# Row by row on ScalarE's queue: 33 of 1173 gathered tiles leave GpSimd in a graph network on one core

## The chip, the cores and the metric

The kernel runs on one core of a Trainium2 chip. The metric is the device time of one execution in microseconds, and the time before is the median of three runs. A core has five engines, each with a queue of instructions of its own that it takes in order: TensorE (PE, matrix products, with weight loads as PEld), VectorE (DVE), ScalarE (ACT), GpSimd (POOL) and SyncE (SP, which only starts transfers). A "q" behind an engine's name (ACTq, DVEq) stands for its sequencer, which loads registers, waits for semaphores and issues transfers.

## The reference

The program is a graph network of three layers over N = 6250 nodes with D = 256 features, and E = 100000 edges, each with a source, a destination, one of R = 3 relations and 32 attributes. Edges are sorted by destination.

```python
ew = edge_attr @ edge_w + edge_b                       # [E, 256], the same in all layers
inv_cnt[i] = 1 / max(number of edges of relation i that end in a node, 1)
for l in range(3):
    residual = x
    msg = relu(x[src] * ew)                            # a row of x for each edge
    out = 0
    for i in range(3):
        h = segment_sum(msg * (edge_type == i), dst)   # [6250, 256]
        out += (h * inv_cnt[i]) @ weights[l, i]
    out += x @ roots[l] + biases[l]
    x = residual + relu(out)
return layernorm(x_in + x)
```

The part that matters here is `x[src]`: for each edge, in each layer, one row of 256 floats (1 KB) has to come from the table x in memory, at an index known only at run time.

## The kernel before

**Tiles.** Edges are cut into tiles of 128. Two tiles are a pair, and a layer has 391 pairs. Two pairs share a room, a tile `xs` of 128 x 2 x 2 x 256 floats (`room`, 8 of them, so 16 pairs). The order of pairs in a layer is fixed in `schedule`. An inner loop runs over iterations `it`; in each, every step of the pipeline acts on a pair that is some places ahead or behind.

**One iteration, in the order of the program.** The whole kernel is written under a manual schedule: each engine does its own instructions in exactly this order.

- `gather` / `gather_pair` (L898 to L902) for the pair nine places ahead: two indirect transfers on POOL's queue. Each reads 128 indices from `src_io` and fetches 128 rows of 1 KB into half of a pair's place in the room. POOL does nothing else in the loop. A gather has to wait until the room's previous content has been reduced.
- Transfers on SP's queue: attributes `at` for eight pairs (L559), weights, and, where a block of nodes ends, its rows of x for the next layer (`x_mid`, L723) or the output.
- `reduce` (L640 to L647) for the current pair: PE multiplies the weighted rows `xs` by one-hot matrices `oh` into `h_p`, which has two buffers. With it, sums over edges become matrix products.
- `make_ew` (L594 to L606), in every fourth iteration: PE computes `ew` of four pairs into four banks `ew_p`.
- `add` (L649 to L659) for the pair before: DVE adds `h_p` to `acc`, at a place that it holds in a register. Registers are loaded eight at a time (L652, a TENSOR_LOAD on DVE's sequencer).
- `weigh` (L623 to L628), in every second iteration, for the room that is three pairs ahead: DVE multiplies each pair's 128 x 512 values by its `ew_p` (L626, reading and writing `xs`), and ACT does one relu over the room (L628).
- For each block of 128 nodes, spread over the iterations: `root_turn` (PE), `root_turned` (L668, an ACT copy `t_s`), `root_mul` (L672, PE) and `root_keep` (L675, DVE) for x @ roots; `node_mul` (L687, PE), `node_end` (L718, L721, DVE) and `clear` (L704, ACT) for the sums that are complete.
- `one_hot` (L630 to L638) for the room two places ahead: four DVE comparisons, and in layer 0 a copy on ACT (`oh_b`, L638).

ACT's queue carries few transfers in the loop: nine pieces of x (L545 to L548) and one block of indices (L564) in layer 0.

**Between layers.** The rows that layer l + 1 gathers are those that layer l has written to `x_mid`; the first pairs of a layer are gathered early and completed by `complete` (L612 to L621).

Of the kernel before, what the change touches and what calls it, by code (L numbers as in the profile page):

```python
# [8 lines left out]
F32 = mybir.dt.float32  # L9
BF = mybir.dt.bfloat16  # L10
I32 = mybir.dt.int32
# [431 lines left out]
def ordered_path(ctx, tc, x, attr_laid, A, weights, roots, biases, edge_w, edge_b, out, src, src_i, seg, place_i, consts, x_root,  # L443
# [6 lines left out]
    nc = tc.nc  # L450
    P = 128
    N, D = x.shape
# [10 lines left out]
    order, _, moved, least, most = schedule(N, E, 1)  # L463
# [19 lines left out]
    with tc.tile_pool(name="bias_s", bufs=1) as bias_s:  # L483
# [9 lines left out]
        rows_of = bias_s.tile([P, D], F32, name="rows_of")  # L493
# [34 lines left out]
    edge = ctx.enter_context(tc.tile_pool(name="edge", bufs=2))  # L528
# [7 lines left out]
    def first_of(p, n):  # L536
        return p == 0 or order[p - 1] // n != order[p] // n
# [19 lines left out]
    def load_at(g):  # L557
        at = edge.tile([P, GROUP // OCT, 2, P], F32, name="at", bufs=3)
        nc.sync.dma_start(at.rearrange("p o i e -> p (o i e)"), attr_laid[g])  # L559
        return at  # L560

    def find_came():
        e = 2 * P * order[0]
        nc.scalar.dma_start(came_i.rearrange("p t e -> p (t e)"),  # L564
                            src[e:e + 2 * FIRST * P][None, :].to_broadcast([P, 2 * FIRST * P]))
        for t in range(2 * FIRST):
            nc.vector.tensor_scalar(came[:, t, :], came_i[:, t, :], node_i[:, 0:1], None, op0=ALU.is_equal)

    def layer(l, r_sb, b_sb, ats, early, pools):
# [5 lines left out]
        x_rows = x if l == 0 else x_mid[l - 1]  # L575
        w_sb = wpool.tile([P, R * DC, D], F32, name="w_sb")
        CH = DC + 1 if l == 0 else DC
        xs, ew_ps, ohs, h_ps, o_ps, rs = {}, {}, {}, {}, {}, {}
        x0s, mvs, oh_bs, t_ss, places = {}, {}, {}, {}, []
        r_next, ats_next, early_next = (None, None), {}, {}  # L580

        def gather(u):
            p = order.index(u)
            if p < FIRST:
                xs[u // 2] = early[u // 2]
            else:
                if first_of(p, 2):
                    xs[u // 2] = room(rows, D)
                gather_pair(nc, xs[u // 2], x_rows, src_i, u)

        def pairs_of(q):
            return range(min(2, U - 2 * q))
# [15 lines left out]
        def gather_early(p):  # L608
            u = order[p]
            if first_of(p, 2):  # L610
                early_next[u // 2] = room(rows, D)
            gather_pair(nc, early_next[u // 2], x_mid[l], src_i, u)  # L612

        def complete(q):
            for k in pairs_of(q):
# [4 lines left out]
                                     start=True, stop=True)  # L620
                nc.vector.tensor_add(xs[q][:, k], rest, xs[q][:, k])  # L621

        def weigh(q, pairs=None):  # L623
            pairs = pairs_of(q) if pairs is None else pairs
            for k in pairs:
                nc.vector.tensor_mul(xs[q][:, k], ew_ps[2 * q + k], xs[q][:, k])  # L626
            there = xs[q][:, pairs.start:pairs.stop]
            nc.scalar.activation(there, there, AF.Relu)  # L628

# [112 lines left out]
        def load_x0(c):  # L742
            n = min(P, N - c * P)
            x0s[c] = edge.tile([P, D], F32, name="x0", bufs=2)
            if n < P:
                nc.vector.memset(x0s[c], 0.0)
            nc.sync.dma_start(x0s[c][:n, :], x[c * P:c * P + n, :])
# [12 lines left out]
        for it in range(-11, max(starts) + 7):  # L760
            def pair(k):
                return order[it + k] if 0 <= it + k < U else None
            if pair(AHEAD) is not None:
                gather(pair(AHEAD))
            if l < L - 1 and 0 <= it + AHEAD - U < FIRST:
                gather_early(it + AHEAD - U)
            if l == 0 and it == 20:
                find_came()
            if pair(AHEAD) is not None and pair(AHEAD) // GROUP not in ats:
                ats[pair(AHEAD) // GROUP] = load_at(pair(AHEAD) // GROUP)  # L770
            if l == 0 and it >= -4 and (it + 4) % 20 == 0 and (it + 4) // 20 * 6 < NT - 1:
                load_x((it + 4) // 20 * 6)
            if it == 10:
                nc.sync.dma_start(w_sb, weights[l].rearrange("r (c p) e -> p (r c) e", p=P))
            if l == L - 1 and it + 2 in root_at:
                load_x0(root_at[it + 2])
            if l < L - 1 and it == U - 10:
                r_next = load_root(l + 1)
            if l < L - 1 and U - 10 <= it < U - 8:
                ats_next[at_groups[it - U + 10]] = load_at(at_groups[it - U + 10])  # L780

            if pair(0) is not None:
                reduce(pair(0))
            if pair(4) is not None and first_of(it + 4, OCT):
                make_ew(pair(4) // OCT)
            if pair(-LAG) is not None:
                add(pair(-LAG))
            if pair(3) is not None and first_of(it + 3, 2):
                if l > 0 and it + 3 < FIRST:
                    complete(pair(3) // 2)  # L790
                if pair(3) // 2 != order[-1] // 2:
                    weigh(pair(3) // 2)

            if pair(3) is not None and pair(3) // 2 == order[-1] // 2:
                weigh(pair(3) // 2, range(pair(3) % 2, pair(3) % 2 + 1))
            if it in root_at:
                root_turn(root_at[it])
            if it - 1 in root_at:
                root_turned(root_at[it - 1])
            if it - 2 in root_at:  # L800
                root_mul(root_at[it - 2])
            if it - 3 in root_at:
                root_keep(root_at[it - 3])
            if it == moved:
                move()
            if it - 2 == moved:
                clear(P)
            if it + 1 in node_at and slot_of(node_at[it + 1]) == 0:
                wrap()
            if it in node_at:  # L810
                node_mul(node_at[it], 0)
            if it - 1 in node_at:
                node_end(node_at[it - 1], 0)
            if it - 2 in node_at:
                node_mul(node_at[it - 2], 1)
            if it - 3 in node_at:
                node_end(node_at[it - 3], 1)
                clear(slot_of(node_at[it - 3]))
            if it - 4 in node_at and l == L - 1:
                deviate(node_at[it - 4])  # L820
            if it - 5 in node_at and l == L - 1:
                norm(node_at[it - 5])
            if pair(2) is not None and first_of(it + 2, 2):
                one_hot(pair(2) // 2)
# [68 lines left out]
def room(rows, D):  # L893

    return rows.tile([128, 2, 2, D], F32, name="xs", bufs=ROWS)


def gather_pair(nc, xs, x_rows, src_i, u):  # L898
    for i in range(2):
        nc.gpsimd.indirect_dma_start(  # L900
            out=xs[:, u % 2, i, :], out_offset=None, in_=x_rows[:, :],
            in_offset=bass.IndirectOffsetOnAxis(ap=src_i[:, 2 * u + i:2 * u + i + 1], axis=0))  # L902
# [162 lines left out]
```

## Time and profile before

| | |
|---|---|
| median of 3 runs | 3694.33 us (3691.32 to 3695.99) |
| the profiled execution | 3692.14 us |
| its span | 3690.3 us |
| its mean granted TensorE clock | 0.843 |
| PE busy | 2687.3 us, 73% |
| DVE busy | 2082.3 us, 56% |
| ACT busy | 935.3 us, 25%, 1155 instructions |
| POOL busy | 2244.9 us, 61%, 2355 instructions |
| DMA, all queues | 387.87 MB, mean 105 GB/s; of that the gathers 307.65 MB |

The page gives for each engine its busy time and its share of the span; instructions of the sequencers are not counted as busy. A group in the page stands for one line, engine, operation and shape, with its number, its busy time, the mean time of one, and the idle time of the engine just before these instructions with what ended most of it. "Issue" as a releaser means that the engine waited for nothing that the profile shows. A releaser "remote" or "another core or an unknown queue" is a semaphore event whose source the profile could not place. PE's ends are modelled, and spans on POOL are rough.

### The profile page before, as it was taken

The page shows a single profiled execution, that of the slowest core. Times are in us where ns is not written, and L with a number is a line of the kernel's source. Part 1 is how long each engine was busy: PE and PEld are TensorE (multiplying, and loading weights), DVE is VectorE, ACT ScalarE, POOL GpSimd, SP SyncE. Part 2 cuts the span into 40 slices and gives each one's busy share as a digit, 9 for nine tenths or more (in the row PEclk, how much of TensorE's full clock was granted, in tenths as well). Part 3 has the DMA queues.
Part 4 walks back from the last instruction along what each step waited for, and adds up shares of the span by engine and source line. Part 5 has one row for each costly group of instructions (what it writes and reads, how often), then busy time and mean ns, then how long its engine had stood idle before and what let it go on. Part 6 is the DMA issues. An engine that isn't in the chain of part 4 may idle for free.

```text
span 3690.3 us, 54932 instructions
## 1 busy us (share of the span) xinstructions
PE 2687.3 (73%) x18875; PEld 2261.2 (61%) x18875; DVE 2082.3 (56%) x5868; ACT 935.3 (25%) x1155; POOL 2244.9 (61%) x2355
## 2 busy tenths in 40 slices
PE   3777877888886667777777777665777777777766
PEld 3666666666666556666666656555666666666655
DVE  4555655566665445555555555544555656666655
ACT  2233333333333222222222222211222222222221
POOL 5666665665566556666666666656666666666664
PEclk9788888888888778888889889787888888888887
DMA  4333333333333333333333333333333333333332
GB/s 129 117 109 119 106 111 98 102 106 103 100 107 106 98 90 100 98 104 104 104 100 106 107 107 104 104 96 112 109 113 113 106 109 111 105 105 107 107 105 67
DMA packets 173323, 387.87 MB, mean 105 GB/s; under 512 B 43418, under 2 KB 78636, under 8 KB 173036
## 3 DMA queue, kind: packets, MB, share of 16 engines
q0 software_dynamic: 112608, 307.65, 28.9%
q1 hardware_dynamic: 53136, 68.50, 5.7%
q10 hardware_dynamic: 7292, 8.11, 0.7%
q8 instruction: 154, 2.52, 0.3%
q14 instruction: 133, 1.09, 0.1%
HBM read 364.62 MB, written 19.46 MB: 104 GB/s over the span
## 4 chain that ended last, share of the span: by engine, by line
PE 49%; another core or an unknown queue 12%; DVE 11%; issue 8%; POOL 1%; DMA 1%; DVEq 1%; ACT 1%; POOLq 0%; ACTq 0%
PE h_p L644 27%; PE o_p L687 10%; PE ew_p L605 6%; DVE xs L626 4%; DVE acc L659 3%; PE r_p L672 3%; PE ew_p L601 2%; DVE x_root L718 2%; DVE oh L634 2%; POOL xs L900 1%; DMA xs<-x_mid,src_io 1%; PE r_p L664 1%; DVE x_all L721 0%; DVEq L659 0%
## 5 line engine op out<-in xcount | busy, mean ns | idle before, releaser
L644 PE MATMUL h_p<-oh,xs 128*128 128x120 f32 x9336 | 1544.9, 317 | 735.5 <-DVE acc L659 485.0
L900 POOL DMA_INDIRECT xs<-x_mid,src_io x1564 | 1497.1, 957 | 930.4 <-issue 810.2
L644 PEld LDWEIGHTS h_p<-oh,xs 128*128 128x128 f32 x9336 | 1400.5, 225 | 916.5 <-DVE acc L659 535.5
L626 DVE TENSOR_TENSOR xs<-ew_p,xs 128x512 f32<-128x512 f32 x1167 | 756.2, 682 | 871.4 <-PE h_p L644 340.3
L628 ACT ACTIVATE xs<-xs 128x1024 f32<-128x1024 f32 (+1 forms) x588 | 617.6, 1050 | 2396.8 <-DVE xs L626 2190.7
L900 POOL DMA_INDIRECT xs<-in_x_dram,src_io x770 | 734.1, 953 | 475.2 <-issue 413.0
L659 DVE TENSOR_TENSOR acc<-h_p,acc 128x240 f32 (+1 forms) x1173 | 518.1, 442 | 448.1 <-remote 255.6
L687 PE MATMUL o_p<-w_sb,acc 128*128 128x256 f32 (+1 forms) x1716 | 523.6, 446 | 109.5 <-DVE x_root L718 57.1
L634 DVE TENSOR_SCALAR oh<-iota_w,seg_o 128x120 f32<-128x120 f32 x2346 | 518.7, 295 | 0.0
L687 PEld LDWEIGHTS o_p<-w_sb,acc 128*128 128x128 f32 (+1 forms) x1716 | 359.0, 223 | 205.8 <-issue 62.9
L605 PE MATMUL ew_p<-ew_sb,at 32*128 32x256 f32 x4692 | 361.8, 426 | 4.4 <-issue 4.4
L605 PEld LDWEIGHTS ew_p<-ew_sb,at 32*128 32x128 f32 x4692 | 275.2, 220 | 42.3 <-issue 12.6
L718 DVE SCALAR_TENSOR_TENSOR x_root<-o_p,inv,x_root 128x256 f32<-128x256 f32 (+1 forms) x429 | 206.0, 480 | 121.6 <-PE o_p L687 42.6
L672 PE MATMUL r_p<-r_sb,t_s 128*128 128x256 f32 x588 | 185.2, 438 | 81.7 <-ACT t_s L668 68.4
L672 PEld LDWEIGHTS r_p<-r_sb,t_s 128*128 128x128 f32 x588 | 113.8, 216 | 104.5 <-ACT t_s L668 74.5
L638 ACT ACTIVATE oh_b<-oh 128x480 bf16<-128x480 f32 x196 | 117.8, 601 | 197.4 <-DVE oh L634 152.2
L704 ACT ACTIVATE acc<-zero_o 128x768 f32<-128x768 f32 (+1 forms) x150 | 140.8, 938 | 74.2 <-PE r_p L687 17.9
L601 PE MATMUL ew_p<-bias,full_ones 3*128 3x512 bf16 x1173 | 142.6, 453 | 21.4 <-issue 17.7
L644 PE MATMUL h_p<-oh_b,full_ones 128*128 128x120 bf16 x782 | 120.1, 238 | 10.0 <-issue 9.6
L644 PEld LDWEIGHTS <-full_ones 128*128 128x128 bf16 x782 | 89.8, 115 | 23.1 <-issue 17.1
L664 PE MATMUL r_p<-ident_o,x_all 128*128 128x128 f32 x294 | 73.2, 340 | 0.0
L675 DVE TENSOR_TENSOR x_root<-r_p,b_sb 128x256 f32<-128x256 f32 x147 | 61.1, 415 | 19.6 <-PE r_p L672 8.5
(92 smaller groups left out, 485.8 us busy)
## 6 DMA issues: line engine op xcount, KB each, us to landing
at<-in_attr_laid_dram SPq DMA_DIRECT2D x147, 256.0 KB
xs<-x_mid,src_io POOLq DMA_INDIRECT x1564
xs<-in_x_dram,src_io POOLq DMA_INDIRECT x770
x_mid<-x_all SPq DMA_DIRECT2D x96, 128.0 KB
x_all<-in_x_dram ACTq DMA_DIRECT2D x8, 768.0 KB
x<-in_x_dram SPq DMA_DIRECT2D x48, 128.0 KB
out_dram<-x_all SPq DMA_DIRECT2D x48, 128.0 KB
w_sb<-in_L_gnn_weights_dram SPq DMA_DIRECT2D x3, 768.0 KB
```

What stands on the lines that cost most here:

```text
L601: nc.tensor.matmul(banks[j].rearrange("p i d -> p (i d)"), full_ones[j * A:j * A + PARTS, :], bias[j * A:j * A + PARTS].rearrange("p i d - ...
L605: nc.tensor.matmul(banks[j][:, i, :], ats[OCT * o // GROUP][j * A:(j + 1) * A, o % (GROUP // OCT), i, :], ew_sb[j * A:(j + 1) * A, :], sta ...
L626: nc.vector.tensor_mul(xs[q][:, k], ew_ps[2 * q + k], xs[q][:, k])
L628: nc.scalar.activation(there, there, AF.Relu)
L634: nc.vector.tensor_scalar(ohs[q][:, t, :], iota_w, seg[:, 4 * q + t:4 * q + t + 1], None, op0=ALU.is_equal)
L644: nc.tensor.matmul(h_ps[u][:, d, :], xs[u // 2][:, u % 2, i, d * P:(d + 1) * P] if d < DC else full_ones, (ohs if d < DC else oh_bs)[u // ...
L659: nc.vector.tensor_tensor(there, h_ps[u][:, :CH].rearrange("p c (r w) -> p c r w", r=R), there, op=ALU.add)
L672: nc.tensor.matmul(rs[c][:, 1, :], t_ss[c][:, d, :], r_sb[:, d, :], start=(d == 0), stop=(d == DC - 1))
L687: nc.tensor.matmul(o_p[:n, j, :], acc[:, d, r, slot:slot + n], w_sb[:, r * DC + d, :], start=(d == 0), stop=(d == DC - 1))
L704: nc.scalar.activation(acc[:, :CH, :, slot:slot + P], zero[:, :, None, None].to_broadcast([P, CH, R, P]), AF.Copy)
L718: nc.vector.scalar_tensor_tensor(root, o_p[:n, j, :], inv[:n, c, r:r + 1], root, op0=ALU.mult, op1=ALU.add)
L900: nc.gpsimd.indirect_dma_start(out=xs[:, u % 2, i, :], out_offset=None, in_=x_rows[:, :], in_offset=bass.IndirectOffsetOnAxis(ap=src_i[:, ...
```

## The change

For 33 of the 1173 tiles of a run (11 in each layer) the gather on POOL is left out. Their rows come one by one: each row is a DMA of its own, 1 KB from the row of x that a register names to one partition of a tile `lent0` (128 x 256 floats, two buffers). ACT's queue issues them.

- `HANDS_OF` lists who fetches rows: one entry, ACT's queue, four rows in an iteration, two buffers.
- `lent_to` plans it: starting in iteration 6, each lent tile takes 32 iterations, one tile after the other. The tile chosen is the first one of a room whose pair stands at least 6 places behind the end of the fetch.
- `lend(it)` is called in each iteration right after `gather`. Four iterations before a tile's fetch begins, SP loads its 128 indices (512 bytes) to one partition. Then four row DMAs are issued in each iteration, and after every eighth row the next eight indices are loaded into ACT's registers. That makes 4224 row DMAs, 528 register loads and 33 index loads in all.
- `gather_pair` skips a lent tile, so one gather of that pair stays.
- `weigh` splits the product of a pair with a lent tile into two products of 128 x 256: the first reads `lent0` and writes to the room, the second works in the room as before. The relu is unchanged.

```diff
@@ layer
+        hands = [(queue, kind, rate, buffers, lent_to(order, N, P, j, rate))
+                 for j, (queue, kind, rate, buffers) in enumerate(HANDS_OF(nc))]
+        lent = {(q, k, i): None for hand in hands for _, q, k, i in hand[-1]}
+        indices, values = {}, {}
+
+        def lend(it):
+            for j, (queue, kind, rate, buffers, plan) in enumerate(hands):
+                for s, q, k, i in plan:
+                    if it == s - 4:
+                        e = (4 * q + 2 * k + i) * P
+                        indices[q] = edge.tile([1, P], I32, name=f"index{j}", bufs=2)
+                        nc.sync.dma_start(indices[q], src[e:e + P][None, :])
+                    if not s <= it < s + -(-P // rate):
+                        continue
+                    if it == s:
+                        lent[q, k, i] = edge.tile([P, D], F32, name=f"lent{j}", bufs=buffers)
+                    for r in range((it - s) * rate, min(P, (it - s + 1) * rate)):
+                        if r % 8 == 0:
+                            _, values[j] = nc.values_load_multi_w_load_instructions(
+                                indices[q][0:1, r:r + 8], engines=[kind], min_val=0, max_val=N - 1,
+                                skip_runtime_bounds_check_because="each source is a node")
+                        queue.dma_start(lent[q, k, i][r:r + 1, :], x_rows[bass.ds(values[j][r % 8], 1), :])
@@ gather
-                gather_pair(nc, xs[u // 2], x_rows, src_i, u)
+                gather_pair(nc, xs[u // 2], x_rows, src_i, u, lent)
@@ weigh
+        def parts(q, k):
+            return [(0, 1), (1, 1)] if any((q, k, i) in lent for i in range(2)) else [(0, 2)]
...
-                nc.vector.tensor_mul(xs[q][:, k], ew_ps[2 * q + k], xs[q][:, k])
+                for i, n in parts(q, k):
+                    there = xs[q][:, k, i:i + n]
+                    rows_of = lent.get((q, k, i))
+                    nc.vector.tensor_mul(there, ew_ps[2 * q + k][:, i:i + n],
+                                         there if rows_of is None else rows_of[:, None, :])
@@ the loop over it
                 gather(pair(AHEAD))
+            lend(it)
@@
+def lent_to(order, N, P, j, rate):
+    steps = -(-P // rate)
+    plan, s = [], 6 + 4 * j
+    while True:
+        p = s + steps + 6
+        while p + 1 < len(order) and (order[p] // 2 != order[p + 1] // 2 or order[p] // 2 == order[p - 1] // 2):
+            p += 1
+        if p + 12 > len(order):
+            return plan
+        q = order[p] // 2
+        plan.append((s, q, j, j))
+        s += steps
+
+def HANDS_OF(nc):
+    return ((nc.scalar, mybir.EngineType.Activation, 4, 2),)
+
+def gather_pair(nc, xs, x_rows, src_i, u, lent=()):
     for i in range(2):
+        if (u // 2, u % 2, i) in lent:
+            continue
         nc.gpsimd.indirect_dma_start(
```

More of the change, by code (lines that the diff above doesn't have):

```diff
@@ L895, in room @@
     return rows.tile([128, 2, 2, D], F32, name="xs", bufs=ROWS)
-def gather_pair(nc, xs, x_rows, src_i, u):
+def lent_to(order, N, P, j, rate):
[13 more added lines that the diff above has]
+def gather_pair(nc, xs, x_rows, src_i, u, lent=()):
     for i in range(2):
+        if (u // 2, u % 2, i) in lent:
+            continue
         nc.gpsimd.indirect_dma_start(
```

## The prediction

> **What bounds the kernel now.** The page is read first, by engine shares, by the chain that ended last and by the costliest groups.
>
> ```profile
> span 3690.3 us, 54932 instructions
> PE 2687.3 (73%) x18875; PEld 2261.2 (61%) x18875; DVE 2082.3 (56%) x5868; ACT 935.3 (25%) x1155; POOL 2244.9 (61%) x2355
> ...
> PE 49%; another core or an unknown queue 12%; DVE 11%; issue 8%; POOL 1%; DMA 1%; DVEq 1%; ACT 1%; POOLq 0%; ACTq 0%
> ...
> L900 POOL DMA_INDIRECT xs<-x_mid,src_io x1564 | 1497.1, 957 | 930.4 <-issue 810.2
> L626 DVE TENSOR_TENSOR xs<-ew_p,xs 128x512 f32<-128x512 f32 x1167 | 756.2, 682 | 871.4 <-PE h_p L644 340.3
> ...
> L900 POOL DMA_INDIRECT xs<-in_x_dram,src_io x770 | 734.1, 953 | 475.2 <-issue 413.0
> ```
>
> By these lines PE would be the bound and POOL idle for over a third. But 930.4 + 475.2 us of idle time "until issue" is no free time, which POOL's timeline shows (columns: start, duration, engine, line, in brackets the idle time before and what ended it).
>
> ```profile
> 1504.41 0.95 POOL L900 DMA_INDIRECT xs<-x_mid,src_io  x1 [2.41 <-issue]
> 1505.66 0.95 POOL L900 DMA_INDIRECT xs<-x_mid,src_io  x1 [0.30 <-issue]
> 1506.91 1.00 POOL L900 DMA_INDIRECT xs<-x_mid,src_io  x1 [0.30 <-issue]
> ...
> 1513.31 0.95 POOL L900 DMA_INDIRECT xs<-x_mid,src_io  x1 [0.30 <-issue]
> 1516.56 0.95 POOL L900 DMA_INDIRECT xs<-x_mid,src_io  x1 [2.29 <-issue]
> ```
>
> A gather costs POOL 0.95 + 0.30 = 1.25 us from start to start. Eight come back to back, four pairs of tiles, and then POOL pauses: 12.15 us a cycle, of which 8 x 1.25 = 10.0 is gathers and about 2.15 is extra pause. So a gather is a term of 1.25, and the question is whether POOL's stream or the PE and DVE work beside it sets 12.15. The view by windows takes whole cycles of POOL, from restart to restart.
>
> ```profile
> core 0: us, PE busy (x) PEld busy (x) DVE busy (x) ACT busy (x) POOL busy (x), PEclk, DMA share, GB/s
> 1504.41:1516.56 12.15, 6.59 (x58) 5.65 (x58) 7.07 (x21) 3.15 (x5) 7.72 (x9) 0.94 0.46 142
> 1516.56:1528.68 12.12, 8.98 (x60) 7.96 (x61) 6.24 (x20) 3.31 (x4) 7.58 (x8) 0.78 0.30 88
> 1528.68:1540.87 12.19, 10.93 (x72) 9.25 (x72) 6.31 (x20) 2.27 (x3) 7.59 (x9) 0.86 0.30 87
> ...
> 3658.90:3676.50 17.60, 16.51 (x131) 14.56 (x132) 15.01 (x47) 5.49 (x6) 0.00 (x0) 0.81 0.01 1
> ```
>
> In the first three rows PE's busy time goes from 6.59 to 10.93 us, the granted clock from 0.78 to 0.94, and the length stays within 12.12 to 12.19. Work that sets a length moves it; PE's does not. POOL's eight gathers are the part that never changes. The last row is the end of layer 2, where no gathers are left, and there PE is busy for 16.51 of 17.60 us. The other half of the handshake is in the chain of waits and in DVE's timeline.
>
> ```profile
> 1510.00 4.30 another core or an unknown queue
> ...
> 1514.32 0.69 DVE L626 TENSOR_TENSOR xs<-ew_p,xs 128x512 f32<-128x512 f32 x1 [4.32 <-remote]
> 1515.70 0.69 DVE L626 TENSOR_TENSOR xs<-ew_p,xs 128x512 f32<-128x512 f32 x1 [0.69 <-remote]
> ...
> 3666.76 0.40 DVE L659 TENSOR_TENSOR acc<-h_p,acc 128x240 f32 x1
> ...
> 3673.97 0.40 DVE L659 TENSOR_TENSOR acc<-h_p,acc 128x240 f32 x1
> ```
>
> DVE stands for 4.32 us, and goes on at 1514.32, just after POOL's last gather of the burst has ended (1513.31 + 0.95 = 14.26); POOL restarts 2.3 later. The last two rows are the first and last of seven adds, one for each pair, from that end of layer 2: 7.21 us in six steps, 1.20 us a pair at a clock of 0.81, against 12.15 / 4 = 3.04 in the steady part. PE and DVE can go twice as fast when POOL is silent, so I read POOL's stream as the pacer and the pause as a fixed toll behind it.
>
> **The change, part by part.**
>
> *Gathers removed.* Each layer lends 11 tiles, 33 in all, so 33 of 2346 gathers go. 33 x 1.25 = 41.3 us off POOL's stream. That they come off singly, one in every eight cycles of a layer, matters: a burst then has seven gathers, and its cycle is 12.15 - 1.25 = 10.90 if the toll stays. Bounds: 41.3 if POOL paces everywhere, 0 if the pause grows by what the burst loses. I take 41.3, because the windows above are nearer to it. The Trainium skill, page "Perfetto Trace Analysis", section "GPSIMD Engine Instruction", says to time such instructions by the spacing of consecutive starts and not by the reported duration; by durations the term would be an estimated 33 x 0.95 = 31 us, and the trace's evenly spaced starts agree with the page.
>
> *What ACT has to do for it.* A lending cycle is four iterations: 16 row DMAs, each with its register step, and two loads of eight registers. There are 3 layers x 11 tiles x 32 / 4 = 264 such cycles. The nearest rows, by source line (ns, least / median / most):
>
> ```profile
> L481 ACTq DMA_DIRECT2D ew_sb<-in_L_gnn_edge_w_dram x4: 337/443/445, 16.1 to 17.5; - x4
> L545 ACTq DMA_DIRECT2D x_all<-in_x_dram x8: 374/375/469, 22.8 to 471.8; - x8
> L652 DVEq TENSOR_LOAD <-place_i x147: 593/597/1049, 52.6 to 3668.5; - x147
> L659 DVEq FUSED_REGOPS  x1170: 69/69/69, 53.3 to 3676.2; - x195
> L1010 SPq FUSED_REGOPS  x1: 186/186/186, 13.5 to 13.5; - x1
> L659 DVEq EVENT_SEMAPHORE  x952: 21/21/1471, 67.3 to 3677.8; - x191
> ```
>
> A row costs an issue of 0.34 to 0.45, a register step of 0.07 to 0.19 and a semaphore wait of 0.02: 0.43 to 0.66. I take 0.443 + 0.069 + 0.021 = 0.53, since L481 is ACT's own run of small loads back to back. A load of eight registers is 0.60. So a cycle costs ACT's queue 16 x 0.53 + 2 x 0.60 = 9.7 us, at most 16 x 0.66 + 1.2 = 11.8. The cycle offers 12.15 (12.0 on the mean of eight once a gather is gone), so I cost it at nothing, but the margin is thin: it is gone from (12.0 - 1.2) / 16 = 0.675 a row. Above that ACT sets the cycle, and each 0.1 us a row costs 16 x 0.1 x 264 = 422 us. The Trainium skill, page "Runtime: NRT & Kernel Launch", section "Instruction fetch mechanics", gives about 200 ns for each register loaded, which speaks against the change: by it the loads would be an estimated 2 x 1.6 = 3.2 us a cycle and the sum 11.7, at the edge. The trace's 597 ns for eight disagrees, and the sum goes by the trace.
>
> *What is queued behind the rows on ACT.* The four rows of an iteration stand ahead of that iteration's relu (L628), t_s copy (L668), clear (L704) and, in layer 0, oh_b copy (L638).
>
> ```profile
> 1516.42 1.06 ACT L628 ACTIVATE xs<-xs 128x1024 f32<-128x1024 f32 x1 [6.46 <-DVE xs L626]
> 1519.35 1.06 ACT L628 ACTIVATE xs<-xs 128x1024 f32<-128x1024 f32 x1 [1.86 <-DVE xs L626]
> 1520.31 0.37 ACT L668 ACTIVATE t_s<-r_p 128x256 f32<-128x256 f32 x1
> 1526.36 1.06 ACT L628 ACTIVATE xs<-xs 128x1024 f32<-128x1024 f32 x1 [5.68 <-DVE xs L626]
> ...
> 1519.04 1.90 PE L644 MATMUL h_p<-oh,xs 128*128 128x120 f32 x8
> ...
> 1524.44 1.05 PE L644 MATMUL h_p<-oh,xs 128*128 128x120 f32 x8
> 1528.43 1.76 PE L644 MATMUL h_p<-oh,xs 128*128 128x120 f32 x8 [2.95 <-DVE acc L659]
> ```
>
> The relus of a cycle's two rooms stand 2.93 us apart and then 7.01. Between them ACT must now issue eight rows and a load, 8 x 0.53 + 0.6 = 4.8 us. The second relu goes to 16.42 + 4.8 = 21.3 instead of 19.35, ends at 22.3, and its reduce runs at 24.44: covered by 2.1 us. The next eight rows end at 26.1, before the next relu at 26.36: on time, by 0.2 us. That relu was released late by DVE, so ACT catches up there. The first room's relu (16.42, reduce at 19.04) has 1.6 us of cover. The t_s copy comes up to 4 x 0.53 = 2.1 later and PE's r_p after it; its cover is PE's idle time of 2.95 at 1528.43. Without these covers each late relu would cost up to 1.9 us a cycle, 264 x 1.9 = 502.
>
> *The DVE product in two.* 33 pairs get two 128x256 products in place of one 128x512 (L626).
>
> ```profile
> L675 DVE TENSOR_TENSOR x_root<-r_p,b_sb 128x256 f32<-128x256 f32 x147 | 61.1, 415 | 19.6 <-PE r_p L672 8.5
> ```
>
> 2 x 0.415 - 0.682 = 0.148 us more, right behind DVE's wait, where it delays the room's relu: 33 x 0.148 = +4.9, as if all of it lay on the path; 0 if the pacing hides it.
>
> *SP.* 33 index loads of 512 bytes, four iterations (12 us) ahead of their first use, on a queue whose transfers in a window of 20 us were these:
>
> ```profile
> 1506.31 0.33 SPq L723 DMA_DIRECT2D x_mid<-x_all  x1
> 1506.73 0.89 SPq L559 DMA_DIRECT2D at<-in_attr_laid_dram  x2
> ```
>
> No wait for them. But the gather that runs beside the second row took 1.00 instead of 0.95, so I charge 33 x 0.05 = +1.7.
>
> *The row transfers themselves.* They bring the same bytes as the gathers did, at 16 KB a cycle. How a gather fares beside them the trace bounds from two sides. Whole cycles with a 768 KB load on ACT's queue (first and third row) against one without:
>
> ```profile
> 98.14:110.36 12.22, 8.81 (x67) 7.82 (x67) 6.43 (x18) 3.52 (x5) 7.67 (x8) 0.78 0.50 152
> 136.22:148.45 12.23, 9.54 (x66) 8.39 (x66) 6.89 (x19) 3.66 (x6) 7.59 (x8) 0.72 0.37 107
> 160.68:172.82 12.14, 9.72 (x67) 8.47 (x67) 6.29 (x18) 3.48 (x5) 7.59 (x8) 0.75 0.49 151
> ```
>
> 12.18 on the mean against 12.23: nothing, or -0.05 a cycle. The other end is the 0.05 us above for each gather, 8 x 0.05 x 264 = +106. I take 0, as ACT's queue is the one that issues here. The tile is used six iterations or more (18 us) after its last row, so DVE does not wait for it.
>
> *Sum.* -41.3 + 4.9 + 1.7 = -34.7. The profiled execution took 3692.1 (span 3690.3), 2.2 under the runs' median of 3694.3; 3692.1 - 34.7 = 3657. With the open bounds: at best 3692.1 - 41.3 - 264 x 0.05 = 3638; at worst, ACT still fitting, 3692.1 + 4.9 + 1.7 + 106 = 3805.
>
> **The rivals.** 0.2% is 7 us, about what a measurement of this kernel can tell from no change.
>
> *POOL's spare time is worth nothing (no change).* POOL waits in every cycle for rooms that PE's reduce frees, so a gather less lengthens the pause. For it: PE has the largest share of the chain. Against it: equal cycles at 6.59 and 10.93 us of PE. Time: 3692 + 4.9 = 3697 or a little less.
>
> *The rows slow the gathers (slower).* Place: POOL's stream in the 264 lending cycles. All 264 x 8 - 33 = 2079 gathers there pay, 33 gain, so it decides from 34.7 / 2079 = 0.017 us a gather. At the 0.05 seen beside SP's issues it is 3657 + 2079 x 0.05 = 3761. For it: two rows' issues fall on every gather, where before most had none, and the toll after the burst, where traffic now never ceases, would need only 34.7 / 264 = 0.13 us more. Against it: the 12.18. The Trainium skill, page "DMA: Bandwidth & Descriptors", section "Issuing engines are not separate DMA queues", says that transfers of all issuers run on the same 16 DMA engines and interleave; the 0.50 share with no longer cycle shows room there.
>
> *ACT becomes the bound (slower).* Place: ACT's queue, from 0.675 us a row. A register-held address may take two register steps of 0.19 and a dearer issue: at 0.75 a cycle is 13.2, that is 264 x 1.2 = +317, 3974. For it: no row shows an issue with such an address, and the margin is 2.3 us of 12. Against it: all traced pieces at their dearest still give 11.8. At the edge, relus late by parts of a microsecond give 3700 to 3750.
>
> **How the numbers follow.** Forecast 0.47, with its own range 3638 to 3685. No change 0.08. Rows slow the gathers 0.24 (3700 to 3830, and in a tenth of it beyond). ACT as the bound 0.15, of which a third ends under 3830. Partial gain that falls between 3685 and 3700 0.06, split. So faster 0.49, same 0.09, slower 0.42. The range 3638 to 3830 leaves out about 0.1 for ACT far over its budget, 0.03 for strong contention, and 0.03 below.
>
> **What would show it.** In the changed kernel, POOL's timeline has bursts of seven once in eight cycles, and those cycles are near 10.9; the others stay at 12.1 to 12.2. Gathers start 1.25 apart beside ACT's rows; 1.27 or more confirms contention. The source row of the row DMAs shows 0.35 to 0.45 and their register steps 0.07 to 0.19; ACT's relus still wait for DVE. If relus wait for "issue" and cycles are 13 us, ACT is the bound. If seven-gather cycles last 12.15, POOL never paced. I am wrong if a row costs over 0.67, or if a lending cycle grows by 0.13 for any reason.

## The result, and the profile after

The change is slower: a median of 3889.6 us over 6 runs against 3694.4 us before, a ratio of 1.052 (95% interval 1.049 to 1.054). The profiled execution took 3867.4 us, with a span of 3865.5 us.

All times of this section come from chips on which the kernel before takes about 3693 us. The experiments below ran on five chips of two sorts. On three of them the kernel before takes 3693 to 3746 us ("slow chips"), on two 2986 to 2990 us ("fast chips"). Every run is therefore read as a ratio to the kernel before on its own chip. Each chip was used at one time only, so it is not shown that the difference lies in the chip and not in the time.

From the page of the changed kernel (line 604 issues the rows, 601 loads registers, 656 is the DVE product, 659 the relu, 953 the gather):

```profile
span 3865.5 us, 68298 instructions
PE 2768.0 (72%) x18875; PEld 2310.2 (60%) x18875; DVE 2090.3 (54%) x5901; ACT 947.0 (24%) x1155; POOL 2203.5 (57%) x2322
...
L953 POOL DMA_INDIRECT xs<-x_mid,src_io x1542 | 1468.0, 952 | 1064.1 <-issue 913.3
```

The mean of a gather is 952 ns against 957, so the rows do not slow the gathers themselves. What has grown is POOL's idle time, 1064.1 against 930.4 us although 22 gathers of this group are gone. POOL's timeline shows that it sits in the pauses between bursts:

```profile
1541.44 0.95 POOL L953 DMA_INDIRECT xs<-x_mid,src_io  x1 [0.30 <-issue]
1545.23 0.94 POOL L953 DMA_INDIRECT xs<-x_mid,src_io  x1 [2.84 <-issue]
...
1554.00 0.95 POOL L953 DMA_INDIRECT xs<-x_mid,src_io  x1 [0.30 <-issue]
1557.79 0.94 POOL L953 DMA_INDIRECT xs<-x_mid,src_io  x1 [2.84 <-issue]
...
1564.19 0.95 POOL L953 DMA_INDIRECT xs<-x_mid,src_io  x1 [2.96 <-issue]
```

2.84 and 2.96 stand where 2.29 and 2.41 stood, and the last pause comes after three gathers, the fourth of that burst being lent. A pause is here a gap of 0.6 to 8 us between two gathers. Summed over the trace, less the usual 0.30, the pauses take 834 us in 385 places, against 644 us in 324 before: 190 us more. Bursts of four have taken the place of bursts of eight: before there were 86 of four and 235 of eight, after 195 and 158. The view of waits (engine, what waited, for what; total us, times, longest) says who is late. First before, then after:

```profile
ACT xs L628 <- DVE xs L626: 2190.7, 531, 27.8
...
PE r_p L672 <- ACT t_s L668: 68.4, 19, 6.4
```

```profile
ACT xs L659 <- DVE xs L656: 689.8, 170, 29.3
ACT xs L659 <- DMA lent<-x_mid: 655.0, 178, 14.2
...
ACT xs L659 <- DMA lent<-in_x_dram: 215.8, 108, 11.2
...
PE r_p L703 <- ACT t_s L699: 192.8, 83, 5.9
```

Before, 531 relus waited for DVE. After, only 170 do, and for 286 the last event awaited was the landing of a row, on a semaphore that a row DMA ahead of the relu in ACT's queue needed: they come when the queue has its row DMAs out. The relu comes late, the copy t_s comes late, and PE waits three times as long for t_s. ACT has become the bound: of the 3700 us from the first row to the last, its queue stood only 582 us before its own activations (their semaphore instructions, which take part of this in any case, included).

Why, when its pieces are cheap? The view of lines 604 and 601 (ns, least / median / most):

```profile
L604 ACTq FUSED_REGOPS  x4224: 2/37/1067, 76.4 to 3776.5; - x192
L604 ACTq MOVE lent<-x_mid x2816: 2/29/758, 1381.6 to 3776.5; - x188
L604 ACTq DMA_DIRECT2D lent<-x_mid x2816: 2/228/786, 1381.6 to 3776.6; - x188
```

```profile
L601 ACTq TENSOR_LOAD <-index x528: 3/720/942, 75.8 to 3773.2; - x176
```

At the medians a row is 0.037 + 0.029 + 0.228 us and some 0.1 between them, 0.39 in all; a load of eight registers is 0.72. The medians hide one thing: the first row behind a load takes 0.461 us to issue, not 0.228 (the median of those 528 rows). So a load costs 0.98 us with the gaps around it, and a load and its eight rows take 4.12 us, the median of the 528 groups. That is 2 x 4.12 = 8.2 us in a lending cycle, less than predicted. Two things come on top, and ACT's and SP's timelines show both:

```profile
1548.73 4.39 ACTq L604 DMA_DIRECT2D lent<-x_mid  x7
1553.17 1.06 ACT L659 ACTIVATE xs<-xs 128x1024 f32<-128x1024 f32 x1 [5.75 <-DMA xs<-x_mid,src_io]
...
1560.46 3.21 ACTq L604 DMA_DIRECT2D lent<-x_mid  x8
```

```profile
1546.96 0.34 SPq L754 DMA_DIRECT2D x_mid<-x_all  x1
1547.40 0.40 SPq L559 DMA_DIRECT2D at<-in_attr_laid_dram  x1
```

*Waits for semaphores that SP holds.* Eight rows take 3.21 us when nothing is in the way. The row behind SP's store had its registers ready at 1547.2 and issued at 1548.73. By the trace's semaphores it used the one that the store of 1546.96 had, and the row at 1550.93 the one that the load of 1547.40 had. Transfers of SP and ACT share eight semaphores in turn, and each waits for the one before it on the same semaphore. Summed over the trace, 196 rows waited so for 350 us, 1.3 us a lending cycle.

*Slow stretches.* The maxima of 758 to 1067 ns belong to stretches in which one instruction after the other takes about 0.7 us, register steps that wait for nothing among them. In the 157 full cycles of eight gathers, 411 of the rows' instructions on ACT's queue took over 0.5 us, and all but one of them started between 4 and 11 us after the burst's first gather. The transfers that the page counts as instructions (queue q14, 237 of 8 KB, before 133) do not explain them: in these 7 us, 26% of the slow instructions and 29% of all the rows' instructions lie within 3 us of one. Over the rows' own instructions the excess sums to some 500 us (190 in durations against the medians, 320 in gaps of over 0.5 us before a register step or without an SP transfer on the semaphore), 1.9 us a lending cycle. 8.2 + 1.3 + 1.9 = 11.4, and the waits and hand-overs of ACT's activations come on top: the 12.0 that the cycle offers are about full.

### The profile page after: what moved, and what is told of

The parts are those of the page before. It is cut to its first block, busy times and chain, and to the rows that moved or that the text cites. A ratio compares the mean times of both kernels' runs of the same rounds, so it can differ in the third digit from the quotient of the medians.

```text
span 3865.5 us, 68298 instructions
## 1 busy us (share of the span) xinstructions
PE 2768.0 (72%) x18875; PEld 2310.2 (60%) x18875; DVE 2090.3 (54%) x5901; ACT 947.0 (24%) x1155; POOL 2203.5 (57%) x2322
## 5 line engine op out<-in xcount | busy, mean ns | idle before, releaser
L953 POOL DMA_INDIRECT xs<-x_mid,src_io x1542 | 1468.0, 952 | 1064.1 <-issue 913.3
L675 PE MATMUL h_p<-oh,xs 128*128 128x120 f32 x9336 | 1566.0, 320 | 655.9 <-issue 326.6
L675 PEld LDWEIGHTS h_p<-oh,xs 128*128 128x128 f32 x9336 | 1426.2, 228 | 850.0 <-issue 444.1
L953 POOL DMA_INDIRECT xs<-in_x_dram,src_io x759 | 721.8, 951 | 557.9 <-issue 427.2
L656 DVE TENSOR_TENSOR xs<-ew_p,xs 128x512 f32<-128x512 f32 (+1 forms) x1167 | 743.2, 675 | 529.2 <-remote 270.4
L718 PE MATMUL o_p<-w_sb,acc 128*128 128x256 f32 (+1 forms) x1716 | 532.3, 452 | 84.7 <-issue 31.4
L703 PE MATMUL r_p<-r_sb,t_s 128*128 128x256 f32 x588 | 234.5, 535 | 236.4 <-ACT t_s L699 192.8
L703 PEld LDWEIGHTS r_p<-r_sb,t_s 128*128 128x128 f32 x588 | 136.1, 256 | 285.5 <-ACT t_s L699 215.5
L699 ACT ACTIVATE t_s<-r_p 128x256 f32<-128x256 f32 x147 | 55.9, 380 | 302.5 <-DMA lent<-x_mid 112.2
```

What stands on the lines that cost most here:

```text
L656: nc.vector.tensor_mul(there, ew_ps[2 * q + k][:, i:i + n], there if rows_of is None else rows_of[:, None, :])
L675: nc.tensor.matmul(h_ps[u][:, d, :], xs[u // 2][:, u % 2, i, d * P:(d + 1) * P] if d < DC else full_ones, (ohs if d < DC else oh_bs)[u // ...
L703: nc.tensor.matmul(rs[c][:, 1, :], t_ss[c][:, d, :], r_sb[:, d, :], start=(d == 0), stop=(d == DC - 1))
L718: nc.tensor.matmul(o_p[:n, j, :], acc[:, d, r, slot:slot + n], w_sb[:, r * DC + d, :], start=(d == 0), stop=(d == DC - 1))
L953: nc.gpsimd.indirect_dma_start(out=xs[:, u % 2, i, :], out_offset=None, in_=x_rows[:, :], in_offset=bass.IndirectOffsetOnAxis(ap=src_i[:, ...
```

## The experiments

Three theories were set against each other: lanes (ACT waits for semaphores that SP holds; a lane is one of the eight), sequencer (ACT has too much to do), and contention (row transfers slow gathers or PE). All kernels but one start from the changed one. The runs on which the readings rest:

| run | chip, before | median | ratio (95%) |
|---|---|---|---|
| no rows | 3693 | 3658.5 | 0.991 (0.990 to 0.992) |
| rows on SP's queue | 3693 | 3947.6 | 1.070 (1.068 to 1.072) |
| rows, all gathers kept | 3693 | 3891.4 | 1.056 (1.053 to 1.060) |
| fixed rows | 3693 | 3735.7 | 1.011 (1.010 to 1.013) |
| fixed rows, one DMA of four | 3694 | 3677.4 | 0.996 (0.994 to 0.997) |
| the same | 2990 | 2951.3 | 0.987 (0.985 to 0.988) |
| two rows an iteration | 3694 | 3749.2 | 1.015 (1.013 to 1.017) |
| the same | 2990 | 2971.1 | 0.994 (0.993 to 0.996) |
| half-length gathers, rows | 3746 | 3944.9 | 1.053 (1.051 to 1.055) |
| half-length gathers, no rows | 3746 | 3736.9 | 0.998 (0.997 to 0.999) |
| the same eight registers throughout | 2986 | 2949.3 | 0.988 (0.986 to 0.989) |
| the change again | 3694 | 3881.1 | 1.052 (1.050 to 1.053) |
| the change again | 2986 | 3074.2 | 1.031 (1.028 to 1.033) |

**Nothing fetched.** `lend` does nothing, and the 33 tiles are a tile of zeros.

```diff
-                        lent[q, k, i] = edge.tile([P, D], F32, name=f"lent{j}", bufs=buffers)
+                        lent[q, k, i] = empty
...
-                        queue.dma_start(lent[q, k, i][r:r + 1, :], x_rows[bass.ds(values[j][r % 8], 1), :])
```

> The 33 gathers are left out and nothing fetches their rows: those 33 tiles are taken as zeros, so the output is not the reference's; the split products stay. If POOL's stream paces the steady part, as the prediction had it: 3694 - 41 + 5 = 3658 us. If POOL's spare time is worth nothing: 3694 to 3699. Every theory of what the rows cost (lanes, ACT's sequencer, contention) expects the same of this run; it gives the base from which the rows' cost is counted.

3658.5 us: the gathers were worth what the prediction said. A burst of seven and the restart after it:

```profile
941.77 0.95 POOL L951 DMA_INDIRECT xs<-in_x_dram,src_io  x1 [2.55 <-issue]
943.03 0.95 POOL L951 DMA_INDIRECT xs<-in_x_dram,src_io  x1 [0.31 <-issue]
...
952.77 0.95 POOL L951 DMA_INDIRECT xs<-in_x_dram,src_io  x1 [2.48 <-issue]
```

952.77 - 941.77 = 11.0 us; the median of the 20 cycles with seven gathers is 10.82. POOL paces, and the pause stays. Fetching the rows costs 3889.6 - 3658.5 = 231 us.

**SP's queue in place of ACT's.**

```diff
-    return ((nc.scalar, mybir.EngineType.Activation, 4, 2),)
+    return ((nc.sync, mybir.EngineType.SP, 4, 2),)
```

> The same rows, fetched by SP's queue in place of ACT's; everything else as in the change. Lanes (ACT's rows wait for the semaphore lanes that SP's stores and loads hold, and hold up the relus) and sequencer (ACT has not the time for rows, register loads and its own work): both expect the loss to go, 3655 to 3690 us, with SP's own stores and loads a little later. Contention (row transfers slow the gathers or PE): the loss stays, 3850 to 3900.

3947.6 us, worse than on ACT, and no theory had said so. SP has nothing to compute, and still becomes late. Its register step in the view of the line, and a wait of PE that hardly exists otherwise:

```profile
L604 SPq FUSED_REGOPS  x4224: 2/37/1398, 32.4 to 3857.4; - x192
```

```profile
PE ew_p L629 <- DMA at<-in_attr_laid_dram: 192.2, 51, 9.9
```

The slow stretches follow the rows to SP's queue, with up to 1.4 us an instruction, and what is late is now the load of `at` that stands behind the rows. So the relu behind the rows is not the root: both queues that were tried fall behind, and each has something on it that is needed in time.

**Gathers kept, rows fetched besides.**

```diff
-                gather_pair(nc, xs[u // 2], x_rows, src_i, u, lent)
+                gather_pair(nc, xs[u // 2], x_rows, src_i, u)
```

> All gathers stay, and ACT fetches the 33 tiles' rows besides, into tiles that nobody reads; no product is split. If a gather that is left out is worth 1.25 us, 3890 + 36 = 3925 us; if it is worth nothing, 3885 to 3890. If the rows only hurt because DVE waits for them (the product reads a tile that comes too late), the loss would be gone: 3694.

3891.4 us, as with 33 gathers fewer. Where ACT is the bound, a gather less is worth nothing. DVE's use of the fetched tile is not the cause either, since nobody reads it here.

**Fixed rows.**

```diff
-                        queue.dma_start(lent[q, k, i][r:r + 1, :], x_rows[bass.ds(values[j][r % 8], 1), :])
+                        queue.dma_start(lent[q, k, i][r:r + 1, :], x_rows[r:r + 1, :])
```

> The same row DMAs on ACT's queue, but each from a fixed row, without registers (so the output is not the reference's): no register loads, no index loads, no register steps. Lanes: the waits behind SP's transfers stay, 3840 to 3890 us. Sequencer: 2 x 0.75 + 16 x 0.1 = 3.1 us of ACT's time in each of 264 cycles goes, and with it most of the loss, 3670 to 3730. Contention: 3850 to 3890.

The register loads and the index loads are gone too. 3735.7 us: of 231 us, 154 go with the registers, their loads and the index loads, and 77 stay. The waits behind SP's transfers are all there (some 230 of them, 353 us), so where ACT has time to spare these waits cost 77 us at most; where it has none they may cost more. ACT has time here: from the first row to the last its queue stands 1899 of 3577 us before its activations, against 582 of 3700 in the change. The slow stretches have gone from the rows: in the whole trace no row's issue took over 493 ns.

> As the run with fixed rows (3736 us), but one DMA of four rows in each iteration in place of four of one row: the same bytes to the same partitions with a quarter of the issues and of the lane uses. If the 77 us that fixed rows still cost are issues and waits in lanes behind SP's transfers: 3658 to 3680. If they are the row traffic beside the gathers: 3730 or so.

> One DMA of four fixed rows an iteration on ACT's queue (the output is not the reference's). On the chip of 2990 again 2951. On the chip of 3693: 3658 to 3680 if the cost of fixed rows is in issues and lanes, 3730 or so if it is in the row traffic.

This is one DMA of four fixed rows in each iteration (`lent[q, k, i][r:r + 4, :]` from `x_rows[r:r + 4, :]`). On the slow chip it took 3677 us, 19 over no rows, and the waits behind SP's transfers fall to 6 us. So 58 of the 77 us go with the number of issues and the semaphore waits, and at most 19 are row traffic. On the fast chip all of the gathers' worth is kept.

**Register loads alone, and fixed rows with register loads.** The row DMA is left out, or its address is fixed, and the loads stay in the program.

> As the run without rows (33 gathers gone, the tiles taken as zeros), but with the 33 index loads and the 528 loads of eight registers on ACT; no row DMAs. In the change a register load took 0.72 us, two a cycle. ACT's sequencer as the bound: 1.5 us of 12 is within its time, 3658 to 3670 us. If a register load itself holds more than its 0.72 us (it stalls ACT, or the memory that it reads from), 3720 or more.

> Also repeated for the other chip: register loads and index loads alone, no row DMAs, 33 gathers gone. On the chip of 3693, against 3658 without them: 3658 to 3670 if 1.5 us more on ACT in a cycle of 12 are hidden, 3720 or more if register loads stall ACT beyond their 0.72 us.

> The run with fixed rows (3736 us), to which the 33 index loads and the 528 register loads are given back; only the two register steps before each row DMA are still missing (8448 small instructions), and the output is not the reference's. If the number of instructions on ACT's queue makes the slow stretches, 528 more of 4224 do little: 3740 to 3770. If the register loads carry the difference between 3736 and 3890: 3850 to 3890.

> The earlier run of this kernel (fixed rows, register loads and index loads kept, register steps left out) was on the chip of 2990. On the chip of 3693, where fixed rows alone took 3736 and all of the change 3890: 3740 to 3770 if the number of ACT's instructions makes the difference (528 of 8976 come back), 3850 to 3890 if the register loads do.

These four runs did not test what they were meant to: nothing used the registers, and the trace shows the 33 index loads and some 528 waits for a semaphore, but no register load. So the first pair repeats "no rows" (2951.1 us at a ratio of 0.987 on a fast chip, 3710.4 at 0.990 on a slow one). The second pair is fixed rows with the index loads and those semaphore waits: 2969.2 at 0.992 (0.991 to 0.994) and 3829.8 at 1.021 (1.019 to 1.024). The latter is 0.010 above fixed rows alone, some 37 us, though on another slow chip, and its rows wait about twice as long behind SP's transfers (719 us against 353). So not all of the 154 us can be laid to the registers.

**Half the rate.** Two rows an iteration, 15 tiles in all (`Activation, 2, 2`).

> The change with two rows an iteration in place of four: 5 tiles a layer, 15 in all, 1920 rows. At the 1.05 us a gather that the run without rows showed, 15 gathers are worth 16 us: 3677 if the rows cost nothing. ACT's sequencer as the bound (in the change 8.1 us a cycle of its own work, 2.8 us in slow stretches, 1.3 us in lanes): half of all that fits into 12 us, 3675 to 3715. A fixed price for each row (231 / 4224 = 0.055 us, contention): 3677 + 105 = 3782.

> Two rows an iteration, 15 tiles, as in the run before. On the chip of 2990 again 2971. On the chip of 3693: 3677 if the rows cost nothing, up to 3715 if slow stretches still reach ACT, 3782 at a fixed price for each row.

On the fast chip 18.5 us are gained, which is 15 x 1.25 = 18.8: the rows are free there. On the slow chip it is 3749 us, 72 over the 3677 that was expected of free rows. Here ACT is mostly in time (470 relus wait for DVE), and POOL's pauses still take 731 us, against 644 without rows. It is PE that waits longer, for nothing that the profile shows. The run without rows, and this one:

```profile
PE h_p L673 <- issue: 259.6, 289, 19.1
```

```profile
PE h_p L675 <- issue: 376.8, 449, 21.0
```

The same wait with four rows in one DMA on a slow chip, with fixed rows on a slow chip, and in the change on a fast chip:

```profile
PE h_p L672 <- issue: 261.8, 321, 25.7
```

```profile
PE h_p L671 <- issue: 354.9, 410, 25.7
```

```profile
PE h_p L675 <- issue: 27.5, 26, 3.1
```

So on slow chips this wait grows by some 100 us where the rows are issued one by one, and not where a quarter as many DMAs bring as many rows. That fits the 72 us here and the 77 of fixed rows, but no run isolates it. How rows on ACT's queue delay PE on a slow chip stays open.

**Half the bytes in every gather.** 512 bytes a row in as many gathers, with the row DMAs and without. The products then read the half that came twice, in two instructions of half the size, which DVE has to do besides.

```diff
-            out=xs[:, u % 2, i, :], out_offset=None, in_=x_rows[:, :],
+            out=xs[:, u % 2, i, :128], out_offset=None, in_=x_rows.rearrange("n (h d) -> (n h) d", h=2)[:, :],
```

> The change, with every gather cut to 512 bytes a row: as many gathers and as many rows, half the bytes; the products read the half that came twice, in two instructions (so the output is not the reference's). To be compared with the run that has the same short gathers and no rows. On the chip of 3693, if the gathers' bytes in flight make the stretches in which other engines issue slowly: the pauses of POOL shrink and the row DMAs cost much less than the 231 us that they cost there, under 100 us. If the bytes do not matter: again some 200 us or more over the run without rows. On the chip of 2990: 20 to 40 us over it.

> Gathers of 512 bytes a row, the 33 lent tiles neither gathered nor fetched (taken as zeros). On the chip of 3693: if bytes in flight make the slow stretches and so POOL's pauses, 2950 to 3300 us; if they do not, 3650 to 3700. On the chip of 2990: 2950 to 2960, POOL's stream alone.

The idea that the gathers' bytes in flight make the slow stretches falls: with half the bytes and no rows the pauses stay (739 us, and a time of 3737), and the rows still cost 3945 - 3737 = 208 us.

**The kernel before, again.** On a slow chip: 3691.4 us, as known. So there is no profile of the kernel before from a fast chip.

> The kernel before, unchanged. The runs so far came from two chips: before took 3693 us on one and 2990 us on the other. On the chip of 3693 this run repeats what is known (bursts of eight gathers and pauses). On the chip of 2990 its profile should show gathers 1.25 us apart without the pause of 2.4 us, since 2334 x 1.25 = 2918 us is nearly all of 2990, and engines that issue at the same pace in all parts of the stream.

**The change, and the same with one register load a layer.** The second keeps every row DMA and its register steps. Three of the 33 index loads stay, and all rows come from the same eight sources of a layer.

```diff
-                        if r % 8 == 0:
+                        if j not in values:
```

> The change, unchanged. On the chip of 3693: 3890 us as before. On the chip of 2990 there should be no slow stretches, so ACT has 8.1 us of its own work and some 1.4 us of lane waits in a cycle of 8 x 1.25 = 10.0 us. If the slow stretches are what makes the change dear: 2960 to 3010 us. If the row DMAs or their lanes are: over 3050.

> The change, unchanged, beside the run with the same eight sources. On chips where before takes 3693 to 3746 us: 1.052 again. On the chip of 2990: 0.990 to 1.010 if the slow stretches are what makes it dear, over 1.02 if the rows or their lanes are.

> The change with three index loads and three register loads in place of 33 and 528 (one a layer): every row DMA still takes its address from a register and has its two register steps, but all tiles use the same eight sources, so the output is not the reference's. As ratios to the kernel before, on chips where that takes 3693 to 3746 us: no rows 0.991, fixed rows 1.011, fixed rows with register loads 1.021, the change 1.052. If the small instructions on ACT's queue carry the difference: 1.035 to 1.050 (3820 to 3880 us at 3693). If register steps are as cheap as their 0.07 us: 1.011 to 1.020. On the chip of 2990, below 1.0.

On a slow chip the change repeats, 3881 us. On a fast chip it is slower too, 3074 us, against an expectation of no more than 1.010. There the slow stretches are absent, as the register step's maximum shows:

```profile
L604 ACTq FUSED_REGOPS  x4224: 37/37/43, 48.3 to 2984.0; - x192
```

So they are not needed to make the change slow. Eight gathers on a fast chip take POOL 8 x 1.25 = 10.0 us without a pause, so ACT has less time: 8.2 us of its own, 1.1 us a cycle behind SP's semaphores (299 us in the trace), and the hand-overs of its activations. Taking away 525 register loads, 2 x 0.98 = 2.0 us a cycle, and 30 index loads brings it under the edge again: 2949 us, all that the gathers are worth. From the first row to the last, ACT's queue then stands 793 of 2805 us before its activations, against 313 of 2936 in the change. That the register loads do it, and not the index loads, is likely and not isolated: fixed rows with all index loads and no register loads took 0.992 on the other fast chip. The waits of the change on the fast chip, and of the kernel with one load a layer:

```profile
ACT xs L659 <- DMA lent<-x_mid: 722.6, 239, 8.7
...
ACT xs L659 <- DVE xs L656: 354.7, 132, 7.1
```

```profile
ACT xs L659 <- DVE xs L656: 1252.8, 402, 6.6
...
ACT xs L659 <- DMA lent<-x_mid: 210.7, 70, 6.9
```

With one load a layer most relus wait for DVE again. How the rest comes about is best seen in one place of the change on the fast chip, in the timelines of ACT, DVE and SP:

```profile
1520.84 10.63 ACTq L604 DMA_DIRECT2D lent<-x_mid  x8
1531.67 1.06 ACT L659 ACTIVATE xs<-xs 128x1024 f32<-128x1024 f32 x1 [10.71 <-DMA xs<-x_mid,src_io]
```

```profile
1523.65 1.28 DVE L656 TENSOR_TENSOR xs<-ew_p,xs 128x512 f32<-128x512 f32 x2
...
1526.72 0.42 DVE L752 SCALAR_TENSOR_TENSOR x_all<-x_root,x_all 128x256 f32<-128x256 f32 x1
```

```profile
1527.17 0.34 SPq L754 DMA_DIRECT2D x_mid<-x_all  x1
1527.61 0.38 SPq L559 DMA_DIRECT2D at<-in_attr_laid_dram  x1
```

The room is multiplied by 1524.9, so its relu could go. But ACT's seventh row has the same semaphore as SP's store of x_mid, and that store waits for DVE's L752, which ends at 1527.1. The row goes out at 1529.0, the eighth behind the `at` load at 1531.2, and the relu 6.7 us late. ACT waited for DVE's work on a finished block of nodes, which the relu does not need.

## Why the prediction was wrong

*Gathers removed, -41.3, and the split product, +4.9: right in sum.* Without rows the time is 3658.5 us where the sum without the index loads was 3656, and a cycle of seven gathers took 10.82 where 10.90 was forecast. That the pause would stay was right for the slow chips; on the fast ones there is no pause, and leaving out the 33 gathers is worth about as much (2989.6 - 2951.1 = 38.5 us).

*What ACT has to do for it: the step that failed.* It said 9.7 us of 12.0, hidden, with the edge at 0.675 us a row. The pieces it priced came out cheaper in sum, 8.2 us: 0.39 a row in place of 0.53, but 0.98 a load in place of 0.60, with the longer issue behind it. What it left out decided. Semaphore waits behind SP's transfers, 1.3 us a lending cycle, were nowhere in the sum: the text said of SP "No wait for them" and looked only at SP's side. And the same instructions take 0.7 us in stretches on a slow chip, which brings another 1.9. The rival "ACT becomes the bound" was what happened, but not from a dearer row, as it had it. That past the edge each 0.1 us a row costs 422 us, as it had it, no run tested. That ACT's queue is what came late is shown by the relus; how its time divides among these terms on a slow chip is worked out from one trace, and is in part argued.

*Registers.* The Trainium skill, page "Runtime: NRT & Kernel Launch", section "Instruction fetch mechanics", gives about 200 ns a register. The 0.72 us for eight, loaded here from a tile on the chip, disagree, at 0.09, or 0.12 with the longer issue behind the load. But the warning was worth more than the row: on the fast chip the loads, with 30 index loads, were the difference between a gain of 1.2% and a loss of 3.1%.

*What is queued behind the rows: half right.* Rows ahead of relu and t_s on one in-order queue were named, with covers of 0.2 to 2.95 us. A single wait of 5 us behind SP goes through all of them.

*The rows slow the gathers: refuted.* Starts within a burst are 1.258 us apart on the mean in the change, 1.262 before. The Trainium skill, page "DMA: Bandwidth & Descriptors", section "Issuing engines are not separate DMA queues", has all transfers interleave on the same 16 engines; here that shows in no gather, and four rows in one DMA leave at most 19 us for traffic.

*What stays open.* On slow chips 154 of the 231 us go when the registers and the index loads go, but the run that splits off the loads exists only for a fast chip. ACT's full queue does not explain all of the loss there: at half the rate, with time to spare on ACT, 1920 rows still cost 72 us, 0.038 each, against 231 / 4224 = 0.055 in the change. The mean granted TensorE clock is lower where the rows cost most, 0.824 in the change's profile against 0.843 before, and 0.904 against 0.93 with one load a layer on the fast chip; whether that is a part of the loss or follows from it was not tested. What makes instructions slow in the second part of a burst was not found. Whether separate semaphores for ACT and SP would save the change was not tried.

## What to carry to other kernels

A queue that issues many small transfers is to be costed as an engine: instructions times their spacing, plus register loads, plus every wait that an in-order queue can inherit. Where transfers share semaphores across queues, as here, the queues are tied together, so list for each new transfer whose completion it waits for, and what that one waits for. Work moved to an idle engine is free only up to the point at which that engine's own few instructions begin to come late, and near that point small parts (here 2.0 us of loads in 10) decide the sign.

## What the runs showed of the hardware

The same kernel takes 2986 to 2990 us on two chips and 3693 to 3746 on three; its mean granted TensorE clock was 0.92 to 0.93 on the former and 0.83 to 0.85 on the latter. On the fast chips POOL gathers without pauses where nothing holds it up, as here with one register load a layer (two gaps of over 0.6 us in the trace, both between layers):

```profile
1507.30 0.95 POOL L953 DMA_INDIRECT xs<-x_mid,src_io  x1 [0.30 <-issue]
1508.55 0.95 POOL L953 DMA_INDIRECT xs<-x_mid,src_io  x1 [0.30 <-issue]
1509.80 0.95 POOL L953 DMA_INDIRECT xs<-x_mid,src_io  x1 [0.30 <-issue]
```

On the slow chips DVE starts little in the second half of each burst, also in the kernel before: of its instructions in the 234 full cycles, 755 start in the first microsecond after the restart and 48 in the eleventh. Whether it lacks work there or is slow, these counts do not tell. In the change, register steps on ACT, which wait for nothing, take about 0.7 us there, and up to 1.1; on SP's queue they took up to 1.4. With half the gathered bytes the rows' cost stayed. How densely instructions stand on the queue matters: of the rows' 12672 instructions in the change 502 took over 0.5 us, at half the rate 49 of 5760, and with fixed rows none of the 4224 issues.
